# A transformer block on one core: how many expert tiles and steps of row maxima each first part gets

## The chip, the cores and the metric

The kernel runs on one core of one Trainium2 chip. The metric is the device time of one execution in microseconds, and its median over the runs. A profiled execution gives the trace from which the views below are taken; its own time is given beside its span.

## The reference

The program computes one block of a transformer with adaptive layer norm. The input x is (4, 2048, 256). With mod = silu(c) @ wmod cut into six rows per batch:

```python
h = layernorm(x) * (1 + ca) + sa
x = x + ga * attention(h)          # 8 heads of 32, causal, softmax over exact row maxima
h = layernorm(x) * (1 + cb) + sb
x = x + gb * experts(h)

# attention: scores = q k^T / sqrt(32) + head_scale * (q[:3].dir) (k[:3].dir)
# experts:   2 shared experts (256 -> 128 -> 256, gelu) for every token, and of 16 routed
#            experts the 4 with the largest softmax(h @ router_w^T), weighted by it
```

All is fp32.

## The kernel before

**Blocks.** The tokens are cut into 16 blocks of 512, four to a batch; qb = i % 4 is a block's place in its batch. A block's queries meet qb + 1 blocks of keys. Attention is done for one group of four heads at a time (NQ = 2 groups) and one key tile of 128 at a time, so block i has ks = 8 (qb + 1) such key tiles to sum, counted over both groups: 8, 16, 24 or 32.

**Maxima.** The exact maximum of every row of scores is found before the exponentials. `maxima(i)` (line 476) gives 8 (qb + 1) steps for a block. A step of `scores` (line 425) makes 4 matmuls of 128 queries by up to 512 keys into two PSUM tiles ps, which TensorE runs as 8; VectorE reduces each of the two tiles into parts, after adding the causal mask cmask to the last 128 columns where the diagonal crosses. The steps of the next block i + 1 are done during block i. Each step carries the time that it is expected to take on VectorE (M_VE = 2.7, and a little more at the start of a row of query tiles); M_US = 1.05 is what it is expected to take on TensorE (line 26).

**Two parts of a block.** The main loop (from the line `for i in range(NBLK)`) does each block in two parts. I call them F i and S i in this document.

- The first part, F i, is a list of pieces of TensorE work, each with a cost in microseconds: the projections of coming blocks (`project_steps`), the output projection of block i - 1 (`out_steps`, PSUM tiles po), the second norm's transposes, the router's logits and the shared experts of block i - 2 (`turn_steps`, `dense_steps`, tiles ptb, pl, pu and pd_s), and tiles of routed experts (`tile_steps`, tiles px, pu and py, four tiles of 128 rows at a time, whose weights wt are loaded by SP's queue). Among them stand steps of maxima of block i + 1.
- The sums, S i, go over the ks key tiles of block i: score matmuls (st), exponentials on ScalarE (p), and two matmuls with the probabilities, for the numerator (av) and the denominator (dv). What is left of the steps of maxima is spread over these key tiles, and VectorE's other work (norms, the router's choice, placing rows for experts) is put between them by `put`, in order, into the room of each key tile.

**The order of work is written out.** Each engine runs its instructions in the order in which the program issues them (class `Pinned`). In a first part, `fill_in` (line 517) decides that order. It keeps a clock t. A piece advances t by its cost. A step of maxima is issued as soon as t is at least free - 0.3 and advances t by M_US; free is then t plus the step's VectorE time. When less than 3 us of pieces is left, the remaining steps are issued one after the other. `fill_in` also calls `tick` at a fixed pace; a tick issues one indirect DMA of the routed experts (a scatter of rows to the experts' buffers, or a gather of results) on POOL, each held behind ScalarE's last instruction by `paced`.

**How much goes into a first part.** Before `fill_in` is called, the loop adds up own (the cost of its own pieces), whole (begin and the VectorE time of all steps of maxima of the next block) and backlog (the cost of all expert tiles that are ready). `take_tiles` takes tiles until the given sum is reached. Then m, the number of steps that are done in this part, is raised while the condition of the `while` loop holds; the rest goes to S i. The expert tiles come in five groups of blocks: [0, 1], [2, 3, 4], [5, 6, 7], [8, 9, 10], [11, 12, 13]. A group's tiles are ready when the last of its rows has been scattered. Blocks 14 and 15 are done at the end with the experts' weights resident.

**The router's choice.** `choice_steps` (line 856) works on the logits of block i - 2: differences to the row maximum, an exponential on ScalarE, shares, the four largest (`choose`), a rank of each row within its expert by small matmuls (`earlier_ones`, PSUM tile pk, which needs VectorE's selb), and weights. `place_steps` (line 1002), for the last block of a group, turns ranks into row addresses. In the kernel before both are put into S i, for every i above 1, ahead of the second norm of block i - 1 (its tiles mvb, rsb and xnb).

**PSUM.** The tiles ps, st and the like come in pairs of banks from a ring of three (`mring`); single banks come from two others (`accp`).

**Combining.** `combine` (line 1217) adds the four gathered rows of a token with their weights into a tile sum, which is stored to the output at the next combine.

Of the kernel before, what the change touches and what calls it, by code (L numbers as in the profile page):

```python
# [12 lines left out]
F32 = mybir.dt.float32  # L13
# [6 lines left out]
P = 128  # L20
# [5 lines left out]
T_US, P_US, M_US, M_VE, S_US = 0.6, 1.8, 1.05, 2.7, 3.2  # L26
# [66 lines left out]
def adaln_block_kernel(  # L93
# [14 lines left out]
    B, T, C = x.shape  # L108
# [34 lines left out]
    work = ctx.enter_context(tc.tile_pool(name="work", bufs=2))  # L143
# [346 lines left out]
    scatters = []  # L490
# [8 lines left out]
    def tick(add=True):  # L499
        for due in sums_due:  # L500
            due[0] -= 1
        if add and sums_due and sums_due[0][0] <= 0:
            sums_due[0][1].pop(0)()
            if not sums_due[0][1]:
                sums_due.pop(0)
        if scatters:
            scatters.pop(0)()
            return
        if not gathers and ready and len(sums_due) < 2:
            gathers.extend(ready[0][0])  # L510
        if gathers:
            gathers.pop(0)()
            if not gathers:
                sums_due.append([3, ready.pop(0)[1]])


    def fill_in(pieces, tops=(), begin=0.0, pace=3.2, add=False):

        pieces, tops = list(pieces), list(tops)
        t, free, turns, next_tick = 0.0, begin, [], 1.0
        while pieces or tops:
            if t >= next_tick:
                tick(add)
                next_tick = t + pace
            if tops and (t >= free - 0.3 or sum(us for us, _ in pieces) < 3.0):
                ve, steps, turn = tops.pop(0)
                t = max(t, free)
                for s in steps:  # L530
                    s()
                t += M_US
                free = t + ve
                if turn is not None:
                    turns.append([3, turn])
                continue
            us, step = pieces.pop(0)
            step()
            t += us
            if turns and us > 0.1:  # L540
                turns[0][0] -= 1
                if not turns[0][0]:
                    turns.pop(0)[1]()
                    t += T_US
        return [turn for _, turn in turns]

    def merged(one, other):

        placed = []
        for pieces in (one, other):  # L550
            at, total = 0.0, sum(us for us, _ in pieces)
            for us, step in pieces:
                placed.append(((at + us / 2) / total, (us, step)))
                at += us
        return [p for _, p in sorted(placed, key=lambda p: p[0])]


    with tc.tile_pool(name="setup", bufs=1) as setup:
# [98 lines left out]
        tops = maxima(1)  # L657
# [537 lines left out]
    def combine_steps(group):  # L1195

        n = group.n

        def gather(j, t, k, held):
            i = group.blocks[j]  # L1200
            at = i * QB + t * P
            if k == 0:
                held["got"] = work.tile([P, TOPK, C], F32, tag="got", name=f"got{i}_{t}")
                held["row"] = work.tile([P, C], F32, tag="row", name=f"row{i}_{t}")
                nc.sync.dma_start(out=held["row"], in_=pre[at : at + P])
            paced(
                nc.gpsimd.indirect_dma_start(
                    out=held["got"][:, k, :],
                    out_offset=None,
                    in_=yg[n % 2][: group.nt * P],  # L1210
                    in_offset=bass.IndirectOffsetOnAxis(
                        ap=group.at[:, j * TT + t, k : k + 1], axis=0
                    ),
                )
            )

        def combine(j, t, held):
            i = group.blocks[j]
            got = held["got"]
            while stores:  # L1220
                stores.pop(0)()
            acc = work.tile([P, C], F32, tag="sum", name=f"sum{i}_{t}")
            held["acc"] = acc
            weight = group.weight[:, j * TT + t]
            nc.vector.tensor_scalar(acc, got[:, 0, :], weight[:, 0:1], None, ALU.mult)
            for k in range(1, TOPK):
                nc.vector.scalar_tensor_tensor(
                    acc, got[:, k, :], weight[:, k : k + 1], acc, ALU.mult, ALU.add
                )

        def complete(j, t, held):
            i = group.blocks[j]
            at = i * QB + t * P
            acc, row = held["acc"], held["row"]
            nc.vector.tensor_tensor(acc, acc, gbs[:, i // NB, :], ALU.mult)
            nc.vector.tensor_tensor(acc, acc, row, ALU.add)
            stores.append(lambda: nc.sync.dma_start(out=of[at : at + P], in_=acc))

        out = []
        for j in range(len(group.blocks)):  # L1240
            for t in range(TT):
                held = {}
                out.append(
                    (
                        [partial(gather, j, t, k, held) for k in range(TOPK)],
                        [partial(combine, j, t, held), partial(complete, j, t, held)],
                    )
                )
        return out
# [126 lines left out]
    def group_of(i):  # L1376
        n = next(n for n, blocks in enumerate(GROUPS) if i in blocks)
        if len(groups) == n:
            groups.append(Group(n, GROUPS[n]))
        return groups[n]  # L1380

    def take_tiles(us):
        got = []
        while tiles_to_come and us > 0:
            got.append(tiles_to_come.pop(0))
            us -= got[-1][0]
        return got
# [16 lines left out]
    for i in range(NBLK):  # L1404
        b, qb = i // NB, i % NB
        ks = NQ * TT * (qb + 1)
        last = i + 1 == NBLK

        if i:
            soon, later = projected_in(i)  # L1410
            outs = out_steps(i - 1, oT)
            turns, ups, downs = [], [], []
            if i > 1:
                turns = turn_steps(i - 2)
                ups, downs = dense_steps(i - 2)
            begin = 5.0
            lead, mid = [], []
            if soon:
                new = project_steps(soon[0])
                lead = new[:2] + turns[:2] + new[2:6]  # L1420
                begin = sum(us for us, _ in lead) + 1.0
                mid = ups + turns[2:] + new[6:]
            elif later:
                new = project_steps(later[0])
                mid = new[:2] + turns[:2] + ups + new[2:3] + turns[2:] + new[3:]
            else:
                mid = turns[:2] + ups + turns[2:]
            if soon and later:
                mid += project_steps(later[0])
            finals = [s for two in zip(downs, outs) for s in two] if downs else outs  # L1430
            at = max(6, len(mid) - len(finals))
            tail = merged(mid[at:], finals) if mid[at:] else finals
            mid = mid[:at] + tail

            for n, s in enumerate(ends):
                (lead or mid).insert(2 * n + 1, (0.001, s))
            tops = [] if last else maxima(i + 1)
            state["pairs"] = not last
            own = sum(us for us, _ in lead + mid)
            whole = begin + sum(ve for ve, _, _ in tops)  # L1440
            backlog = sum(us for us, _ in tiles_to_come)
            now = take_tiles(1e9 if last else max(whole - own, backlog - 90.0))
            filler = own + sum(us for us, _ in now)
            m, busy = 0, begin
            while m < len(tops) and (
                busy + tops[m][0] <= filler + 2.0 or len(tops) - m > int(0.9 * ks)
            ):
                busy += tops[m][0]
                m += 1
            rest = tops[m:]  # L1450
            left = fill_in(lead + (merged(mid, now) if now and mid else mid), tops[:m], begin)
# [20 lines left out]
        for n, (_, ss, turn) in enumerate(rest):  # L1472
            at = int(0.93 * (n + 0.5) / len(rest) * ks)
# [33 lines left out]
            fresh = fresh[1:]  # L1507
        if i > 1:
            group = group_of(i - 2)
            steps = choice_steps(i - 2, group)  # L1510
            if i - 2 == group.blocks[-1]:
                steps += place_steps(group)
                filled = group
            put(steps, 1, 1)
        if i:
            steps = norm(second_norm_steps(i - 1))
# [15 lines left out]
        if 0 < i < 4:  # L1532
            now = tables[:3] if i == 1 else tables[:8]
# [25 lines left out]
    i, j = DENSE  # L1559
# [66 lines left out]
```

## Time and profile before

| | |
|---|---|
| median of 3 runs | 2571.34 us (2566.7 to 2572.5) |
| time of the profiled execution | 2561.29 us |
| its span | 2559.6 us |
| TensorE busy | 2397.4 us, 94% |
| VectorE busy | 1427.1 us, 56% |
| ScalarE busy | 981.4 us, 38% |
| POOL busy | 698.0 us, 27% |
| mean granted TensorE clock | 0.955 |

Busy time is the union of the durations of an engine's instructions. TensorE's matmuls are pipelined and their ends are modelled, so being busy does not mean that it works at its peak: a matmul that is held up or that runs at half the clock counts as busy too. That is why the lengths of the stages are compared in what follows, and not the busy shares. In the rows of the timeline, the first number is the start, the second how long the row lasted; x8 means that eight instructions of the same kind stand in it; the brackets name an idle time of the engine ahead of it and what ended it.

### The profile page before, as it was taken

The page shows a single profiled execution, that of the slowest core. Times are in us where ns is not written, and L with a number is a line of the kernel's source. Part 1 is how long each engine was busy: PE and PEld are TensorE (multiplying, and loading weights), DVE is VectorE, ACT ScalarE, POOL GpSimd, SP SyncE. Part 2 cuts the span into 40 slices and gives each one's busy share as a digit, 9 for nine tenths or more (in the row PEclk, how much of TensorE's full clock was granted, in tenths as well). Part 3 has the DMA queues.
Part 4 walks back from the last instruction along what each step waited for, and adds up shares of the span by engine and source line. Part 5 has one row for each costly group of instructions (what it writes and reads, how often), then busy time and mean ns, then how long its engine had stood idle before and what let it go on. Part 6 is the DMA issues. An engine that isn't in the chain of part 4 may idle for free. (4 is left out here: it accounts for less than half of the span.)

```text
span 2559.6 us, 42608 instructions
## 1 busy us (share of the span) xinstructions
PE 2397.4 (94%) x16961; PEld 1182.3 (46%) x16961; DVE 1427.1 (56%) x2833; ACT 981.4 (38%) x1391; POOL 698.0 (27%) x740
## 2 busy tenths in 40 slices
PE   7989999999999999999999999998999998998987
PEld 4443433345544333365645344364633257335754
DVE  5577665436667774346565656458557840422235
ACT  2324244543333344534343335533342343542420
POOL 3201010421124035201013333502353320354334
PEclk9989899999999899998999999998998999999999
DMA  2300403343532112233622135233623169338943
GB/s 87 118 1 9 148 9 109 115 132 116 163 114 67 34 44 99 73 115 122 211 95 75 50 126 179 82 129 112 221 90 109 56 200 300 110 121 278 325 136 116
DMA packets 219703, 306.91 MB, mean 120 GB/s; under 512 B 18544, under 2 KB 158832, under 8 KB 219504
## 3 DMA queue, kind: packets, MB, share of 16 engines
q1 hardware_dynamic: 192720, 228.89, 27.1%
q0 software_dynamic: 25536, 73.43, 9.0%
q8 instruction: 134, 2.20, 0.4%
q10 hardware_dynamic: 1248, 1.86, 0.2%
q14 instruction: 65, 0.53, 0.1%
HBM read 193.49 MB, written 114.82 MB: 120 GB/s over the span
## 5 line engine op out<-in xcount | busy, mean ns | idle before, releaser
L52 DVE TENSOR_REDUCE parts<-ps 128x2 f32<-128x1024 f32 (+3 forms) x640 | 662.4, 1063 | 318.4 <-PE ps L52 309.3
L52 ACT ACTIVATE p<-st 128x1024 f32<-128x1024 f32 (+3 forms) x640 | 538.6, 893 | 618.8 <-PE st L52 564.4
L52 PE MATMUL st<-qT,kv 32*128 32x512 f32 (+3 forms) x2560 | 412.0, 584 | 15.2 <-ACT p L52 7.6
L52 PE MATMUL ps<-kv,qT 32*128 32x512 f32 (+3 forms) x2560 | 400.8, 614 | 22.1 <-DVE parts L52 11.9
L52 POOL DMA_INDIRECT got<-yg,at x224 | 216.7, 968 | 368.5 <-ACT p L52 96.9
L52 PE MATMUL av<-p,kv 128*32 128x512 f32 (+3 forms) x2560 | 306.6, 549 | 3.8 <-ACT p L52 2.1
L52 PE MATMUL dv<-p,ones 128*32 128x512 f32 (+3 forms) x2560 | 302.3, 541 | 1.5 <-issue 1.5
L72 POOL DMA_INDIRECT xg<-rows,at x219 | 212.8, 972 | 299.5 <-ACT p L52 121.2
L52 PEld LDWEIGHTS st<-qT,kv 32*128 32x128 f32 x2560 | 143.9, 186 | 268.9 <-issue 196.2
L52 DVE TENSOR_TENSOR ps<-ps,cmask 128x256 f32<-128x256 f32 x256 | 109.3, 427 | 253.1 <-PE ps L52 208.6
L52 PEld LDWEIGHTS ps<-kv,qT 32*128 32x128 f32 x2560 | 135.0, 194 | 229.5 <-issue 90.2
L52 POOL TENSOR_TENSOR x<-x,tmps 128x512 f32<-128x512 f32 x28 | 35.4, 1264 | 519.8 <-DVE tmps L52 519.7
L52 PE MATMUL pu<-xt,wt 128*128 128x128 f32 x1216 | 161.3, 283 | 13.9 <-DMA wt<-experts 12.2
L52 PE MATMUL py<-wt,tact 128*128 128x256 f32 x608 | 163.6, 403 | 7.6 <-ACT xt L52 2.1
L52 PEld LDWEIGHTS pu<-xt,wt 128*128 128x128 f32 x1216 | 151.4, 195 | 37.1 <-issue 12.9
L52 PE MATMUL st<-mT,unit 3*128 3x512 bf16 (+3 forms) x1280 | 165.9, 348 | 0.0
L52 PEld LDWEIGHTS dv<-p,ones 128*32 128x32 f32 x2560 | 72.4, 110 | 174.0 <-issue 168.7
L52 ACT COPY y<-py 128x512 f32<-128x512 f32 x152 | 89.0, 585 | 144.1 <-PE py L52 141.5
L52 PEld LDWEIGHTS py<-wt,tact 128*128 128x128 f32 x608 | 111.1, 196 | 50.3 <-issue 9.0
L52 DVE RECIPROCAL rd<-rd 128x128 f32<-128x128 f32 x128 | 120.8, 943 | 0.8
L52 ACT COPY xt<-px 128x512 f32<-128x512 f32 x152 | 86.3, 586 | 85.2 <-PE px L52 82.1
L52 PEld LDWEIGHTS av<-p,kv 128*32 128x32 f32 x2560 | 52.6, 108 | 137.4 <-issue 112.4
(288 smaller groups left out, 2454.0 us busy)
## 6 DMA issues: line engine op xcount, KB each, us to landing
wt<-experts SPq DMA_DIRECT2D x304, 256.0 KB
xr<-xg SPq DMA_DIRECT2D x76, 512.0 KB
yg<-y SPq DMA_DIRECT2D x76, 512.0 KB
xg<-zeros SPq DMA_DIRECT2D x16, 1024.0 KB
xin<-in_x SPq DMA_DIRECT2D x16, 512.0 KB
x<-in_x SPq DMA_DIRECT2D x16, 512.0 KB
h2d<-xnb POOLq DMA_DIRECT2D x14, 512.0 KB
pre<-x POOLq DMA_DIRECT2D x14, 512.0 KB
```

The lines of the kernel that those rows point to most:

```text
L52: made = call(*args, **kwargs)
L72: made = call()
```

## The change

Six things are changed, all of them in the planning code.

- In `fill_in`, ticks follow each other after 2.2 us of its clock while there are scatters, and the next time is set ahead of the call.
- The tile sum has three buffers where the pool gave two.
- For the blocks with qb = 0 (i = 4, 8, 12) `choice_steps` of block i - 2 is merged into the pieces of the first part, two places behind the logits, at 0.05 us each, and is no longer put into the sums. `place_steps` stays in the sums.
- The time to be filled with tiles is reduced by M_US for each step of maxima, and the backlog up to which tiles may wait is 110 us where it was 90.
- The condition on m counts M_US for each step that was already taken, less 5 us, where it had a margin of 2 us.
- For qb = 0 all steps of maxima are done in the first part.

```diff
@@ fill_in
             if t >= next_tick:
+                next_tick = t + (2.2 if scatters else pace)
                 tick(add)
-                next_tick = t + pace
@@ combine
-            acc = work.tile([P, C], F32, tag="sum", name=f"sum{i}_{t}")
+            acc = work.tile([P, C], F32, bufs=3, tag="sum", name=f"sum{i}_{t}")
@@ main loop, first part
+            if i > 1 and qb == 0:
+
+                at = mid.index(turns[2]) + 2
+                steps = choice_steps(i - 2, group_of(i - 2))
+                mid[at:] = merged(mid[at:], [(0.05, s) for _, _, s in steps])
...
-            now = take_tiles(1e9 if last else max(whole - own, backlog - 90.0))
+            idle = whole - own - M_US * len(tops)
+            now = take_tiles(1e9 if last else max(idle, backlog - 110.0))
             filler = own + sum(us for us, _ in now)
             m, busy = 0, begin
+            most = 0 if qb == 0 else int(0.9 * ks)
             while m < len(tops) and (
-                busy + tops[m][0] <= filler + 2.0 or len(tops) - m > int(0.9 * ks)
+                busy + tops[m][0] <= filler + M_US * m - 5.0 or len(tops) - m > most
             ):
                 busy += tops[m][0]
                 m += 1
@@ main loop, sums
-            steps = choice_steps(i - 2, group)
+            steps = choice_steps(i - 2, group) if qb else []
```

## The prediction

> **What bounds the kernel now.** I read the page first, then a table of busy time by stage, then TensorE's timeline inside two stages. The page:
>
> ```profile
> span 2559.6 us, 42608 instructions
> PE 2397.4 (94%) x16961; PEld 1182.3 (46%) x16961; DVE 1427.1 (56%) x2833; ACT 981.4 (38%) x1391; POOL 698.0 (27%) x740
> PEclk9989899999999899998999999998998999999999
> ```
>
> TensorE is busy 94% of the span, VectorE 56%. The change adds no matmul and takes none away, so it can only alter how fast TensorE gets through its queue. I cut the span where a block's first score matmul (st) starts and its last denominator matmul (dv) ends: F i is the first part of block i, S i its sums. In each row, after the stretch: its length, then busy us of PE, PEld, DVE, ACT, POOL, the granted clock, DMA share, GB/s.
>
> ```profile
> 795.90:844.20 48.30, 44.82 (x196) 23.86 (x196) 33.20 (x42) 9.89 (x16) 10.28 (x10) 0.89 0.17 52
> 844.20:957.00 112.80, 110.57 (x893) 35.35 (x893) 82.26 (x159) 44.40 (x55) 28.59 (x31) 0.95 0.11 37
> 1189.60:1302.00 112.40, 105.38 (x624) 69.44 (x620) 71.63 (x100) 38.09 (x65) 13.40 (x15) 0.95 0.65 209
> 1302.00:1349.90 47.90, 47.02 (x501) 16.57 (x499) 27.35 (x92) 29.32 (x39) 10.97 (x14) 1.00 0.05 16
> 1401.60:1513.70 112.10, 109.75 (x893) 34.69 (x893) 67.94 (x119) 44.41 (x54) 40.42 (x44) 0.97 0.19 63
> 1561.40:1661.10 99.70, 98.37 (x947) 30.67 (x946) 55.31 (x152) 60.30 (x71) 49.49 (x52) 1.00 0.36 108
> 1763.20:1865.20 102.00, 89.74 (x508) 56.74 (x508) 68.53 (x105) 30.56 (x52) 35.44 (x38) 0.92 0.55 180
> ```
>
> These are F6, S6, F9, S9, S10, S11, F13. S11 holds 32 key blocks and no step of maxima: 99.7/32 = 3.12 us each. S10 holds 24 key blocks and 21 such steps: 112.1 - 24 x 3.12 = 37.3, so **a step costs 1.78 us in a sum**. S7, with five short steps, is 108.5 us: 8.8/5 = 1.76.
>
> What a step costs in a first part, TensorE's timeline of F6 shows (start, us):
>
> ```profile
> 822.24 1.14 PE L52 MATMUL ps<-kv,qT 32*128 32x512 f32 x8
> 823.31 1.99 PE L52 MATMUL pd_s<-wsh,act_-2_6212 128*128 128x256 f32 x8
> 825.14 1.89 PE L52 MATMUL pv<-wq,hT 128*128 128x256 f32 x8
> 826.97 1.99 PE L52 MATMUL ps<-kv,qT 32*128 32x512 f32 x12
> 829.42 1.83 PE L52 MATMUL ps<-kv,qT 32*128 32x512 f32 x8 [0.47 <-DVE parts L52]
> 831.68 0.70 PE L52 MATMUL ps<-kv,qT 32*128 32x256 f32 x4 [0.43 <-DVE parts L52]
> 832.81 7.76 PE L52 MATMUL ps<-kv,qT 32*128 32x512 f32 x24 [0.43 <-DVE parts L52]
> 840.50 3.73 PE L52 MATMUL po<-wo,oT 128*128 128x256 f32 x8
> ```
>
> Each step is 8 ps rows. Between other work it takes 1.07 us (822.24 to 823.31), and its two reductions (1221 ns each in the groups) run under the pieces that follow. When the pieces have run out, steps stand in a row: six from 826.97 to 840.50, 13.5 us, **2.26 us each**, at VectorE's pace. So there are three prices: 1.07 spread, 1.78 in a sum, 2.26 in a row. Granted clock in two such rows (F6 and F14):
>
> ```profile
> 827.00:840.50 13.50, 12.15 (x49) 4.42 (x48) 12.23 (x13) 0.59 (x1) 1.53 (x2) 0.75 0.28 87
> 1935.50:1954.60 19.10, 16.91 (x73) 7.10 (x72) 18.19 (x22) 0.00 (x0) 8.58 (x9) 0.73 0.38 122
> ```
>
> **The change, part by part.** *Allotment.* The new idle takes M_US off per step, so fewer tiles go into each first part; the new m adds M_US per step, so more steps do. fill_in is not changed: it still issues a step only when t reaches free, and free is the end of the step's matmuls plus its VectorE time. Each step thus still wants about 2.7 us of pieces. With fewer pieces per step the pieces run out earlier, and the rest of the steps stand in a row. I carried out the planner's arithmetic and read the order of matmuls on TensorE. Steps in each first part, in brackets those in a row at its end, and us of pieces:
>
> F4, F8: 16 (3), 63 -> 16 (6), 47. F5: 21 (3), 66 -> 21 (7), 53. F6: 11 (6), 26 -> 23 (8), 55. F9: 24 (3), 80 -> 21 (7), 53. F10: 11 (3), 34 -> 30 (12), 67. F12: 16 (2), 63 -> 16 (7), 46. F13: 21 (3), 66 -> 21 (8), 53. F14: 11 (9), 14 -> 29 (11), 67. F3, F7: 3 -> 1; F11: 8 -> 6 (short steps). F15 keeps 76 of 80 tile pieces.
>
> Tile pieces cost TensorE the same wherever they stand (F9: 112.4 less its steps is 83 for 80 planned), so moving them sums to nothing. They take their DMAs along: each set of four tiles has four weight loads of 256 KB, a row load and a store of 512 KB on SP's queue. They move from F9 (209 GB/s) to F10 and F14 (60 and 161 GB/s now); I cost it at 0, for F15 with 283 GB/s loses only some 10 us to late weights. If that cover fails the nearest row is those 10 us; below nothing, at most the same 10.
>
> Steps, all in us. Rows: 35 steps now, measured 73.1 in all (6.9 twice, 5.6, 13.5, 6.2, 5.8, 3.5, 5.6, 19.1). After: 72. Priced by VectorE's durations (2.28 a full step; with the causal edge 1.69 to 3.15) they make 165.8; short rows now cost up to 1.7 less than their VectorE sum and long ones none or 0.7, so I take 161: +88. Spread steps rise from 112 to 121: 9 x 1.07 = +10. From the sums 49 long steps go (12 in S6, 19 in S10, 18 in S14) and 3 come (S9): 46 x 1.78 = -82. Six short ones leave F3, F7 and F11 (0.63 each, -4) and come to S3, S7, S11 (1.76 each, +10.5). **Sum of the steps: +22.5.**
>
> *Clock.* After a row the last pieces run slow: po took 3.73 us at 840.50, against 1.99 for the same x8 of pd_s at 823.31. After the rows of F5, F10, F12 and F13, now two or three steps long, it shows no such slowing. Those four become long, and F6's gets one more piece behind it: some 1.8 for each, I take +8. The Trainium skill, "TensorE: Matmul & The Clock Gate", section "HAM oscillation — how this bites in real kernels", asks only for no TensorE gap over some 3.4 us; in the row at 827 no gap is over 0.47 us, and the clock still fell to 0.75. By the rule the term is 0 and the total +12; I go by the row. Ends: 0 and +15.
>
> *Choice.* choice_steps of blocks 2, 6 and 10 goes from S4, S8, S12 to F4, F8, F12: about 25 small VectorE instructions (some 5.5 us), one Exp, ten small pk matmuls and a copy. In S12 it stands ahead of place_steps on VectorE, and the second norm's power (rsb) comes behind both. F13 pays for it:
>
> ```profile
> 1775.65 0.48 PE L52 MATMUL ptb<-ident,xnb 128*128 128x128 f32 x1 [4.20 <-POOL xnb L52]
> ```
>
> Three more waits of 1.0 follow, 7.3 in all, under a half clock. Without the choice the chain starts some 5.5 us earlier: -6.5 in F13, -1 in S12. S4 and S8 gain nothing (TensorE idles 0.2 there). In F4, F8, F12 the Exp stands among Gelu tiles, and the program has six more table loads, 1.28 us each in the trace, 7.7 on ScalarE; copies that TensorE waits for stand behind. Half, +4. Queued behind pk are all of TensorE's pieces: if VectorE is late with selb, everything waits. Three steps lie between logits and need, so I take 0; ends 0 and +7 for each of three (the wait of F13).
>
> *Rest.* S14 costs 7 more than S10 now: 21 steps and nine combines on one VectorE (90.1 of 119.1). With 3 steps left: -5. F11's first row load waits 3.3; older tiles now stand ahead of it: -2. The third sum buffer: VectorE waits 34.8 for out<-sum, mostly in the end, where TensorE's gaps name other causes: 0; ends 0 and -3. Scatters every 2.2 instead of 3.2 (40 in F10) are 0.97 each on a POOL that is busy 18 of F10's 52: 0; a late POOL would show as x or xnb, up to +3.
>
> **Sum:** +22.5 + 8 - 7.5 + 4 - 5 - 2 = **+20 us**. The profiled execution took 2561.29 (span 2559.6 and 1.7 around it), so 2581. It lies 10 under the median of the runs, 2571.34; with that offset the forecast is 2591.
>
> **The rivals.** *A, faster: the rows cost less.* The new formula treats both engines as working side by side. If the steps in a row cost 1.66 (halfway between 1.07 and 2.26) the 72 make 120 instead of 161: 20 - 41 = -21, 2550. It decides at 20/72 = 0.28 less, about 1.96 us a step. For it: rows of three now stay under their VectorE sum. Against: at six, seven (16.1 in F1) and nine steps they don't, since the ps pairs are three, one and a half steps. *B, no change:* no clock term, no table loads, a little off the rows: about 2574. *C, much slower:* pk or the Exp holds up F4, F8 and F12 as the late norm holds up F13, 7 and a half-clock stretch of 3 each: 3 x 10 more, 2621. Against it: VectorE is busy only 48 of 85 us in F4, though 54 of 72 afterwards.
>
> **Numbers.** Forecast 0.62 (its own range 2578 to 2606), A 0.17, B 0.11, C 0.10. What a measurement here can tell from no change is about 0.2%, 5 us. A is faster, B counts as no change with a little of A's and the forecast's edges in balance, the rest is slower: 0.17, 0.10, 0.73. The range 2556 to 2616 leaves out the lower half of A and the upper half of C, and the far ends of the forecast.
>
> **What would show it.** Right: S10 near 78 us, S6 near 92, S14 near 82; F10 near 116, F14 near 110, F6 near 93; rows of 7 to 12 steps at 2.2 us, with the clock at about 0.75; F4 and F8 some 12 shorter, not 17; ptb's wait in F13 mostly gone. Wrong: rows under 1.9 us a step, or none; S5 and S9 much slower than 57 and 55; pk waiting over 2 us.

## The result, and the profile after

| | before | after |
|---|---|---|
| median of 5 runs | 2571.21 us (2566.7 to 2572.5) | 2584.65 us (2581.46 to 2586.71) |
| ratio to before | 1 | 1.0064 [1.0045, 1.0083] |
| profiled span | 2559.6 us | 2585.0 us |
| mean granted clock | 0.955 | 0.946 |

The change costs 0.64%. The profiled run of before lies 10 us below its median and that of after at the top of its runs, so the traces differ by 25.4 us where the medians differ by 13.4. The ratio, 0.64% or 16 us, is not that of the two medians (0.52%). The page of after:

```profile
span 2585.0 us, 42615 instructions
PE 2409.9 (93%) x16961; PEld 1195.0 (46%) x16961; DVE 1431.2 (55%) x2833; ACT 987.5 (38%) x1397; POOL 700.2 (27%) x740
PEclk9989899998999899999999899989899999998999
```

TensorE has the same number of matmuls and is busy 93% of the span in place of 94%; ScalarE has the six more instructions that the prediction named as table loads. So the answer is again in the stages. The first seven rows answer to those shown of before (F6, S6, F9, S9, S10, S11, F13); then come F10, F14, S14 and the end E, which is all that follows S15. The columns are those of before. The second table has F10, F14, S14 and E of before.

```profile
780.60:869.60 89.00, 84.28 (x456) 49.84 (x456) 62.14 (x75) 23.98 (x42) 4.57 (x4) 0.94 0.31 101
869.60:959.80 90.20, 88.30 (x798) 28.75 (x798) 53.00 (x123) 44.96 (x56) 40.61 (x44) 0.98 0.27 86
1183.50:1269.60 86.10, 79.97 (x441) 47.98 (x438) 58.09 (x76) 25.32 (x42) 6.30 (x7) 0.95 0.49 158
1269.60:1323.10 53.50, 52.58 (x524) 18.11 (x523) 34.19 (x98) 27.39 (x38) 10.99 (x13) 0.99 0.04 14
1442.40:1519.80 77.40, 76.48 (x739) 24.67 (x738) 22.88 (x65) 44.80 (x55) 14.77 (x17) 1.00 0.16 52
1552.90:1656.60 103.70, 102.85 (x963) 31.99 (x962) 60.38 (x159) 58.47 (x69) 56.11 (x59) 1.00 0.37 111
1754.20:1850.80 96.60, 84.99 (x443) 52.14 (x440) 66.93 (x100) 23.95 (x40) 36.36 (x38) 0.88 0.55 180
...
1323.10:1442.40 119.30, 111.24 (x588) 67.28 (x589) 81.15 (x100) 31.55 (x55) 44.24 (x45) 0.87 0.56 182
1905.20:2015.10 109.90, 104.32 (x616) 66.26 (x612) 77.96 (x95) 31.28 (x56) 13.56 (x13) 0.92 0.65 210
2015.10:2098.10 83.00, 79.26 (x748) 25.41 (x747) 48.20 (x120) 44.92 (x56) 40.72 (x44) 1.00 0.29 88
2303.80:2585.00 281.20, 233.81 (x1050) 164.12 (x1048) 103.01 (x230) 72.04 (x114) 109.37 (x115) 0.91 0.64 210
```

```profile
1349.90:1401.60 51.70, 48.28 (x235) 28.37 (x234) 32.11 (x38) 13.62 (x22) 17.92 (x18) 0.93 0.18 60
1920.50:1956.50 36.00, 33.02 (x152) 17.66 (x152) 31.50 (x38) 4.17 (x7) 15.21 (x15) 0.86 0.48 161
1956.50:2075.60 119.10, 114.23 (x893) 35.51 (x893) 90.10 (x172) 44.30 (x54) 39.82 (x43) 0.94 0.20 58
2288.00:2559.60 271.60, 231.39 (x1050) 163.42 (x1048) 102.97 (x230) 71.97 (x114) 109.10 (x115) 0.93 0.66 217
```

F6, F10 and F14 grew by 40.7, 67.6 and 73.9 us; S6, S10 and S14 shrank by 22.6, 34.7 and 36.1. F9 lost 26.3 and S9 gained 5.6. These are moves of steps and tiles, and most of them cancel. What does not cancel is how the steps stand in the first parts. TensorE's timeline at the end of F10 (start, duration; the brackets name the idle time ahead of the row and who ended it):

```profile
1410.26 1.13 PE L52 MATMUL py<-wt,tact 128*128 128x256 f32 x4 [0.29 <-ACT xt L52]
1411.32 1.35 PE L52 MATMUL ps<-kv,qT 32*128 32x512 f32 x12
1413.78 0.49 PE L52 MATMUL ps<-kv,qT 32*128 32x128 f32 x4 [1.11 <-DVE parts L52]
1414.91 23.36 PE L52 MATMUL ps<-kv,qT 32*128 32x512 f32 x80 [0.64 <-DVE parts L52]
1438.19 3.41 PE L52 MATMUL po<-wo,oT 128*128 128x256 f32 x8
```

From 1411.3 to 1438.2 TensorE issues nothing but ps: 96 matmuls, 8 to a step, so twelve steps in 26.9 us, 2.24 us each, at VectorE's pace. Nine first parts have such a row (F4, F5, F6, F8, F9, F10, F12, F13, F14), of 6, 7, 8, 6, 7, 12, 7, 8 and 11 steps: 72 steps in 159.8 us, where before had 35 in 73.1. Busy time and clock in the rows of F10, F14 and F4:

```profile
1411.30:1438.20 26.90, 25.15 (x98) 10.63 (x97) 25.49 (x30) 0.59 (x1) 10.59 (x11) 0.61 0.22 74
1986.30:2011.00 24.70, 22.68 (x89) 9.19 (x88) 23.95 (x28) 0.59 (x1) 8.95 (x9) 0.72 0.40 133
601.00:614.90 13.90, 12.57 (x50) 4.89 (x49) 12.53 (x16) 1.87 (x2) 0.00 (x0) 0.64 0.34 114
```

VectorE is busy 25.5 of 26.9 us in F10's row: it, not TensorE, sets the length, although TensorE too shows as busy. The granted clock is 0.61 to 0.72, and the po behind F10's row takes 3.41 us.

The other loss was not foreseen: E is 281.2 us where it was 271.6. TensorE in E, two rows of after, the row of before that answers to the second, and then two of after's scatters on POOL ahead of it:

```profile
2327.91 5.41 PE L52 MATMUL pd<-kv,act 128*128 128x256 f32 x16 [1.90 <-DVE act L52]
2347.37 1.94 PE L52 MATMUL px<-ident,xr 128*128 128x128 f32 x8 [14.05 <-DMA xr<-xg]
```

```profile
2325.18 1.94 PE L52 MATMUL px<-ident,xr 128*128 128x128 f32 x8 [8.11 <-DMA xr<-xg]
```

```profile
2321.02 0.96 POOL L72 DMA_INDIRECT xg<-rows,at  x1 [2.32 <-ACT gates L52]
2326.88 0.96 POOL L72 DMA_INDIRECT xg<-rows,at  x1 [4.90 <-ACT act L52]
```

The first routed tile of the end waits 14.05 us for its rows (8.11 before), and those rows wait for scatters that are held behind ScalarE's last instruction.

### The profile page after: what moved, and what is told of

Read it like the earlier page. It is cut to its first block, busy times and chain, and to the rows that moved or that the text cites. A ratio compares the mean times of both kernels' runs of the same rounds, so it can differ in the third digit from the quotient of the medians.

```text
span 2585.0 us, 42615 instructions
## 1 busy us (share of the span) xinstructions
PE 2409.9 (93%) x16961; PEld 1195.0 (46%) x16961; DVE 1431.2 (55%) x2833; ACT 987.5 (38%) x1397; POOL 700.2 (27%) x740
## 3 DMA queue, kind: packets, MB, share of 16 engines
q1 hardware_dynamic: 192720, 228.89, 26.9%
## 4 chain that ended last, share of the span: by engine, by line
PE 78%; DVE 8%; issue 4%; ACT 4%; DMA 3%; POOL 1%; another core or an unknown queue 1%; SPq 0%; POOLq 0%; ACTq 0%; DVEq 0%
PE st L52 16%; PE ps L52 14%; PE av L52 10%; PE dv L52 9%; PE pu L52 6%; PE py L52 5%; DVE parts L52 4%; PE po L52 2%; PE ppq L52 2%; DMA wt<-experts 2%; PE pv L52 2%; PE px L52 2%; PE ppk L52 2%; PE pd_s L52 2%; POOL got L52 1%
## 5 line engine op out<-in xcount | busy, mean ns | idle before, releaser
L52 PE MATMUL ps<-kv,qT 32*128 32x512 f32 (+3 forms) x2560 | 439.4, 649 | 26.4 <-DVE parts L52 19.3
L52 PE MATMUL st<-qT,kv 32*128 32x512 f32 (+3 forms) x2560 | 391.6, 582 | 12.9 <-ACT p L52 9.9
L52 PEld LDWEIGHTS ps<-kv,qT 32*128 32x128 f32 x2560 | 156.6, 203 | 250.7 <-issue 106.2
L52 PEld LDWEIGHTS st<-qT,kv 32*128 32x128 f32 x2560 | 132.7, 185 | 257.7 <-issue 192.0
L52 PE MATMUL py<-wt,tact 128*128 128x256 f32 x608 | 165.7, 404 | 10.9 <-ACT xt L52 3.2
L52 PE MATMUL st<-mT,unit 3*128 3x512 bf16 (+3 forms) x1280 | 152.4, 346 | 0.0
L52 DVE SCALAR_TENSOR_TENSOR sum<-got,weight,sum 128x256 f32<-128x256 f32 x168 | 84.3, 502 | 93.9 <-DMA got<-yg,at 81.7
L52 POOL TENSOR_TENSOR x<-x,tmp 128x512 f32<-128x512 f32 x32 | 41.0, 1283 | 316.9 <-DVE tmp L52 277.7
```

The costliest lines, as they stand in the source:

```text
L52: made = call(*args, **kwargs)
```

## The experiments

Each kernel has 5 to 12 runs. The chips differ (the medians of before were 2561.17 us for e1 to e4, 2554.78 for e5 to e8, 2550.49 for e9 to e12), so only the ratios to before on the same chip are compared. A ratio's interval, in brackets, reaches 0.15 to 0.3% to either side. The stages come from one profile of each kernel, and the clock alone moves them: S0 has the same matmuls in all fourteen kernels and is 32.7 us long in before and after, granted 1.00, but 37.3 in e11, granted 0.85. A stage's difference of up to some 5 us means little unless a wait or a second profile goes with it.

### Which part of the change costs what: e1, e2, e3

**e1: the change without the move of the choice.**

```diff
-            if i > 1 and qb == 0:
-                at = mid.index(turns[2]) + 2
-                steps = choice_steps(i - 2, group_of(i - 2))
-                mid[at:] = merged(mid[at:], [(0.05, s) for _, _, s in steps])
...
-            steps = choice_steps(i - 2, group) if qb else []
+            steps = choice_steps(i - 2, group)
```

> The changed kernel with choice_steps put back into the sums for every block; all else as changed. Rows theory (the loss is made by steps of maxima that stand one after the other at the end of a first part, at VectorE's pace): the rows stay (7, 7, 8, 7, 7, 12, 7, 8, 11 steps), so it stays slower than the kernel before, within 6 us of the changed kernel, 2579 to 2590. Choice theory (the router's choice among the pieces, with its wait of pk and its table loads, makes the loss): 2571 or less.

Measured: 2603.85 us, 1.0170 [1.0144, 1.0197]. Both expectations missed, on the same side: without the choice's move the change would cost 1.70%. The move is worth 1.06% in it, some 27 us. Where, TensorE's timeline at the start of F9 shows, first of e1, then of after:

```profile
1193.25 0.45 PE L52 MATMUL ptb<-ident,xnb 128*128 128x128 f32 x1 [0.90 <-DVE rd L52]
1193.94 0.47 PE L52 MATMUL ptb<-ident,xnb 128*128 128x128 f32 x1 [0.25 <-POOL xnb L52]
1195.43 0.48 PE L52 MATMUL ptb<-ident,xnb 128*128 128x128 f32 x1 [1.01 <-POOL xnb L52]
1196.91 0.47 PE L52 MATMUL ptb<-ident,xnb 128*128 128x128 f32 x1 [1.01 <-POOL xnb L52]
```

```profile
1188.08 0.63 PE L52 MATMUL ptb<-ident,xnb 128*128 128x128 f32 x4
```

In e1 the second norm is so late that its first four transposes are issued one by one, the last three each when POOL hands over its xnb. This is the wait that the prediction had seen in F13 alone. In after the four stand in one row without a wait. From the start of F5, F9 and F13 to the first ps TensorE takes 15.6, 15.4 and 19.9 us in e1, and 8.2, 8.2 and 14.9 in after. Against e1, after is shorter by 5.7 us in F5, 7.2 in F9, 6.3 in F13 and 2.5 in S12, together 21.7 of the 27. (The profiled spans differ by 11.5 only: S3 and E of after are 4.7 and 4.6 longer, stages whose work the edit leaves as it is.)

**e2: only the move of the choice, on the kernel before** (the same lines, added).

```diff
+            if i > 1 and qb == 0:
+                at = mid.index(turns[2]) + 2
+                steps = choice_steps(i - 2, group_of(i - 2))
+                mid[at:] = merged(mid[at:], [(0.05, s) for _, _, s in steps])
...
-            steps = choice_steps(i - 2, group)
+            steps = choice_steps(i - 2, group) if qb else []
```

> The kernel before with nothing but choice_steps moved to the first parts of blocks 4, 8 and 12. Rows theory: the rows of F4, F8 and F12 stay at two steps, S12 and F13 gain some 7, pk and the table loads take about 4 back: 2564 to 2574, no slower than before. Choice theory: 2580 or more.

Measured: 2535.06 us, 0.9902 [0.9876, 0.9928], a gain of 25 us where about nothing was expected. By stages of the two profiles: F13 -4.6 and S12 -2.0, near what was predicted, but also F5 -4.5, F9 -1.5, F10 -1.7, and F4 -4.2, F8 -4.5 and S4 and S8 -0.8 and -1.1, where the prediction had a cost or nothing. F4 and F5 of e2, and then of before:

```profile
535.90:616.60 80.70, 76.87 (x442) 48.71 (x442) 49.24 (x93) 32.02 (x52) 5.12 (x5) 1.00 0.51 169
637.90:726.40 88.50, 84.80 (x512) 54.46 (x508) 58.34 (x76) 30.62 (x52) 6.28 (x7) 1.00 0.49 159
```

```profile
536.80:621.70 84.90, 80.81 (x430) 50.01 (x428) 47.69 (x72) 29.12 (x48) 5.18 (x5) 0.96 0.50 163
643.80:736.80 93.00, 87.41 (x516) 56.02 (x512) 62.67 (x90) 30.74 (x52) 12.17 (x14) 0.96 0.48 152
```

Both are granted the full clock, where before had 0.96 in each. The two gain in different ways. F5, F9 and F13 gain at their start, as in the change: the first ps comes after 7.3, 8.5 and 14.6 us, where before took 11.8, 10.9 and 19.1. F4 and F8 gain at their end. The choice's pieces advance the clock of `fill_in` too, so one step more is spread, and the row is two steps long and not three. The last ps of F4's row and the po behind it, of before and of e2:

```profile
614.96 3.12 PE L52 MATMUL ps<-kv,qT 32*128 32x512 f32 x8 [0.21 <-DVE parts L52]
618.01 3.78 PE L52 MATMUL po<-wo,oT 128*128 128x256 f32 x8
```

```profile
613.62 1.13 PE L52 MATMUL ps<-kv,qT 32*128 32x512 f32 x4 [0.30 <-DVE parts L52]
614.68 1.99 PE L52 MATMUL po<-wo,oT 128*128 128x256 f32 x8
```

The row is 6.9 us long in before (from 611.1) and 3.5 in e2 (from 611.2); po takes 1.8 us less; the step that is now spread costs 1.0. Together that is F4's gain. So of the 25 us, some 11 lie ahead of the first ps of F5, F9 and F13, where the norm was waited for, and 8.7 in rows that became shorter by a step.

**e3: only the allotment, on the kernel before.**

```diff
-            now = take_tiles(1e9 if last else max(whole - own, backlog - 90.0))
+            idle = whole - own - M_US * len(tops)
+            now = take_tiles(1e9 if last else max(idle, backlog - 110.0))
...
+            most = 0 if qb == 0 else int(0.9 * ks)
...
-                busy + tops[m][0] <= filler + 2.0 or len(tops) - m > int(0.9 * ks)
+                busy + tops[m][0] <= filler + M_US * m - 5.0 or len(tops) - m > most
```

> The kernel before with nothing but the new idle, the backlog of 110 and the new condition on m. Rows theory: rows of 7 to 12 steps as in the changed kernel and no gain in F13: +15 to +28 against before, 2586 to 2599. Choice theory: the loss is gone, 2571 or less, since VectorE's idle time in the first parts takes the steps for nothing.

Measured: 2611.62 us, 1.0177 [1.0145, 1.0209]: 45 us, above the top of what was expected (28); its runs spread from 2595.7 to 2615.9. F5 and F9 of e3:

```profile
641.70:735.20 93.50, 84.58 (x436) 50.52 (x436) 62.30 (x89) 25.56 (x42) 12.15 (x14) 0.88 0.44 140
1195.30:1288.60 93.30, 83.54 (x436) 50.04 (x436) 62.31 (x89) 25.55 (x42) 12.17 (x14) 0.89 0.45 146
```

F5 has 13 us of pieces less than in before and takes 0.5 more; the prediction's steps and tiles had it 7.6 shorter. F9 is 19.1 shorter and not 25.5, F12 3.2 and not 10. S3, to which two short steps come, priced at 3.5, grew by 7.4. Together that is 25 us over the forecast. S3's part is not the steps': with the same matmuls S3 takes 114.3 us in e1, granted 0.99 and not 0.96. F5, F9 and F12 are as long in e1 as here. In F5 and F9, 3.7 and 4.5 us of the excess lie ahead of the first ps, which comes after 15.5 and 15.4 us. The clock in F5, F9, F12 and F13 fell to 0.88, 0.89, 0.89 and 0.83, from 0.96, 0.95, 1.00 and 0.92. Length times the share that was not granted is 11.2, 10.3 and 8.3 us in F5, F9 and F12, against 3.7, 5.6 and 0 in before: the clock can account for 20 of the 21 us that these three are over, at most, since in a row TensorE waits anyway. All of these stages follow or hold a row that became long, and the second norm is later: ptb waits 2.3, 2.3 and 9.0 us for xnb in F5, F9 and F13, where in before it waited 1.2, 0.4 and 7.3. That it is F4's and F8's long rows that leave VectorE late for the short S4 and S8 is argued and not shown by itself.

So by ratios: allotment +1.77%; pace and third buffer on top of it -0.07%; choice on top of both -1.06%; sum +0.64%. The second is within the intervals, and cannot be told from nothing.

### Is it the rows: e4, e5

**e4: the change, with TensorE's own time taken off the wait for VectorE.** `fill_in` sets free after t has already advanced by M_US. The edit starts VectorE's time with the step's matmuls, as the new idle and m assume.

```diff
-                free = t + ve
+                free = t + ve - M_US
```

> The changed kernel, with one line of fill_in changed: free = t + ve - M_US, so that a step's VectorE time is counted from its issue and not from the end of its matmuls. The same steps and nearly the same tiles stand in each first part, but spread: at the ends only 2, 2, 3, 2, 2, 5, 3, 0 and 5 steps are left in rows, 24 in place of 72. Rows theory: 48 steps at 1.07 in place of 2.26 and fewer slow clocks, -45 to -65 against the changed kernel, 2520 to 2540. If the rows are not the cause (VectorE or the pairs of ps banks are the bound however the steps are spread): within 10 us of the changed kernel.

Measured: 2514.41 us, 0.9825 [0.9799, 0.9852]; against after's 1.0064 that is 2.4%, 61 us, inside the 45 to 65 expected. The steps in the nine rows fall from 72 to 24. The line also shortens rows that the change had left as they were in before: F0 is 3.8 us shorter than in after and F2 6.2, 10 of the 61. F10 and F14 of e4, and then its timeline inside F10:

```profile
1279.80:1392.80 113.00, 106.25 (x590) 62.84 (x588) 82.07 (x102) 31.70 (x55) 40.30 (x42) 0.92 0.57 188
1836.50:1936.50 100.00, 93.82 (x570) 60.10 (x568) 72.44 (x90) 30.11 (x52) 8.74 (x8) 0.94 0.54 174
```

```profile
1364.82 1.14 PE L52 MATMUL ps<-kv,qT 32*128 32x512 f32 x8
1365.89 1.99 PE L52 MATMUL py<-wt,tact 128*128 128x256 f32 x8
1367.82 1.14 PE L52 MATMUL ps<-kv,qT 32*128 32x512 f32 x8
1368.88 2.05 PE L52 MATMUL pu<-xt,wt 128*128 128x128 f32 x16
```

One step, one piece of 2 us, one step: no wait, and the work between is done in VectorE's time. F10 is 6.3 shorter than in after with the same steps and tiles. (F14 isn't a like comparison: in e4 it has 27 steps and 64 px matmuls, in after 29 and 76, since three scatters of a group come only in F14.) The change's rows are thus not the price of the new allotment by itself, but of a new allotment on an issue rule that was not changed with it.

**e5: the same line on the kernel before.**

```diff
-                free = t + ve
+                free = t + ve - M_US
```

> The kernel before with the one line free = t + ve - M_US in fill_in and nothing else. Its rows shrink from 35 steps to 9 in F4 to F14 (3 in F6, 6 or 7 in F14, none elsewhere), and in F2 from 6 to 3. Rows theory: some 28 steps at 1.07 in place of about 2.1, and the slow clocks behind them, -20 to -40 against before. If what the change adds at the ends of first parts is not the rows: within 5 us of before.

Measured: 2526.31 us, 0.9888 [0.9868, 0.9909], 29 us, as expected. F6 is 3.8 shorter, F10 6.3, F2 6.2, F4 and F8 4.5 each; F11 and F12 give 11.3 and 5.1 back (in F11 the first px waits 6.5 us for its rows, 3.3 in before, and the clock is 0.86 and not 0.93). The line helps without the allotment too, half as much: before had half as many steps in rows. With the line on both sides, the whole change is thus worth 0.9825 against 0.9888, 0.6%.

### What the prediction had costed at nothing: e6, e9, e10

**e6: only the pace of 2.2 us and the third buffer, on the kernel before.**

```diff
+                next_tick = t + (2.2 if scatters else pace)
                 tick(add)
-                next_tick = t + pace
...
-            acc = work.tile([P, C], F32, tag="sum", name=f"sum{i}_{t}")
+            acc = work.tile([P, C], F32, bufs=3, tag="sum", name=f"sum{i}_{t}")
```

> The kernel before with the tick pace of 2.2 while there are scatters and the third buffer of sum, and nothing else. My prediction put both at 0 (ends -3 and +3). Second thought, from the order of instructions: the scatters of the group of blocks 8 to 10 are then all issued in S13, not one late, so that its 80 tile pieces stand in F14 and not in F15, with all 32 steps of maxima of block 15 spread among them: 21 steps leave S14 (-37, and -5 for its combines), F14's row falls from 9 to 3 and 21 more steps come (+16), F15 loses its waits for weights (-10 to -13): about -38. Against it the last fill_in, whose pace was 1.3, becomes slower to scatter: +6 in the end. Sum -25 to -40. If a group's moment does not matter: within 5 us.

Measured: 2509.00 us, 0.9816 [0.9792, 0.9840], 47 us, more than the 25 to 40 expected. F14, S14, F15 and E of e6:

```profile
1907.70:2041.90 134.20, 128.51 (x840) 87.65 (x836) 85.22 (x101) 49.71 (x88) 9.64 (x9) 0.99 0.75 246
2041.90:2114.80 72.90, 72.02 (x723) 23.21 (x722) 41.86 (x114) 44.78 (x55) 40.74 (x44) 1.00 0.40 117
2114.80:2129.00 14.20, 13.39 (x65) 10.17 (x65) 7.47 (x12) 4.18 (x7) 5.75 (x6) 1.00 0.10 29
2229.30:2508.20 278.90, 233.38 (x1051) 163.91 (x1048) 102.93 (x230) 71.99 (x114) 108.77 (x115) 0.92 0.65 211
```

F14 grew by 98.2, S14 and F15 shrank by 46.2 and 96.4: 44 us net. With faster scatters a group's last rows are there before F14 is planned (three of its scatters come in F14 of before, none in F14 of e6), its tiles become pieces of F14 instead of F15, and the steps of maxima stand between them at full clock instead of in S14. E is 7.3 longer. In the change itself this gain is not to be had: there older tiles, left over by the smaller idle and the higher backlog, fill F14 already (64 px matmuls stand in F14 of e3, none in before's).

**e9: the change without the third buffer.**

```diff
-            acc = work.tile([P, C], F32, bufs=3, tag="sum", name=f"sum{i}_{t}")
+            acc = work.tile([P, C], F32, tag="sum", name=f"sum{i}_{t}")
```

> The changed kernel with two buffers of sum, as before. The waits of VectorE for out<-sum come back, mostly in the end, where TensorE waits for other things: the same as the changed kernel, between 0 and +4 us against it (1.003 to 1.009 of before). If the third buffer carries part of what the pace seemed to give: +8 or more.

Measured: 2560.32 us, 1.0034 [1.0017, 1.0051], within what was expected, though on another chip than after's 1.0064; E is 277.3 and the wait of px 13.5. The kernel is not slower without the buffer, so its 0 stands. (Alone on the kernel before, it wasn't tried without the pace.)

**e10: the change with a pace that is never longer than the one it replaces.** In E the old pace was 1.3 us, so 2.2 is slower there.

```diff
-                next_tick = t + (2.2 if scatters else pace)
+                next_tick = t + (min(2.2, pace) if scatters else pace)
```

> The changed kernel with min(2.2, pace) while there are scatters, so that the fill_in of the end, with its pace of 1.3, scatters as before. In the changed kernel its last eleven scatters come 6 us late and the first load of expert rows after them makes TensorE wait 14.1 us in place of 8.1: -5 to -8 against the changed kernel (0.999 to 1.004 of before). If that wait is chance: no change.

Measured: 2555.90 us, 1.0018 [1.0002, 1.0034]. The row of TensorE in E that answers to the one of after:

```profile
2312.56 1.73 PE L52 MATMUL px<-ident,xr 128*128 128x128 f32 x7 [9.82 <-DMA xr<-xg]
```

The wait is 9.82 us instead of 14.05, and E 269.4 instead of 281.2 (277.3 in e9). The other profiles say the same. In the five kernels with 2.2 in the end (after, e1, e4, e6, e9) E is 276.6 to 282.6 us and this wait 12.9 to 15.1; in the nine with 1.3 E is 269.4 to 275.2 and the wait 7.7 to 9.8. So 2.2 in the end costs some 7.5 us, the difference of the means. The ratio is 0.16% below e9's on the same chip; their intervals overlap.

### Is the late norm the whole of the choice's gain: e11

**e11: the kernel before, with the second norm ahead of the choice in S4, S8 and S12.**

```diff
-        if i > 1:
+        for norm_now in ((True, False) if qb == 0 else (False, True)):
+            if not norm_now and i > 1:
...
                 put(steps, 1, 1)
-        if i:
+            if norm_now and i:
...
```

> The kernel before with one order changed: in the sums of blocks 4, 8 and 12 the second norm is put into the key tiles ahead of the router's choice (and of place_steps) and not behind. No work moves to a first part and no row changes. If the choice's gain of 26 comes from the second norm that it held up, F5, F9 and F13 gain 4 to 8 each as in the kernel with the choice alone: -8 to -18. If it comes from the pieces' order in F4, F8 and F12 and their rows of two: within 4 us of before; place_steps coming later could cost up to 3.

Measured: 2555.81 us, 1.0018 [1.0002, 1.0033]: no gain, where 8 to 18 us were expected. The norm does come in time: ptb no longer waits for xnb, and the first ps of F5, F9 and F13 comes after 8.6, 8.5 and 14.4 us, 10 us earlier in all than in before. But S4, S8 and S12 are 5.4, 4.6 and 4.5 longer. TensorE in S12:

```profile
1764.07 0.20 PE L52 MATMUL pk<-selb,earlier 128*128 128x16 bf16 x1 [4.59 <-DVE selb L52]
```

Now the choice is late, and pk holds up everything queued behind it. In neither order do the short sums hold both chains without a wait; moving one of them out is what gains.

### A version that beats both: e7, e8, e12

**e7: everything but the allotment.** Before, with the choice's move of e2, the third buffer, the line of e5 and the pace of e10.

```diff
+                next_tick = t + (min(2.2, pace) if scatters else pace)
                 tick(add)
-                next_tick = t + pace
...
-                free = t + ve
+                free = t + ve - M_US
```

> The kernel before with the choice in the first part, the third buffer, the pace min(2.2, pace) while there are scatters, and free = t + ve - M_US; the allotment stays as before. Rows theory: there is enough filler for every step, so rows vanish but for F1, F2 and F6; choice -26 as measured alone, rows -20 to -30 (part of it is in the -26), group in F14 -30 to -40: -70 to -100 against before, the fastest so far. If the new allotment is what made the spread kernel fast, this one lies above its 0.9825.

Measured: 2471.16 us, 0.9686 [0.9663, 0.9708], 80 us, within the 70 to 100 expected. F14 is 140.7, S14 72.5, F15 14.2 and E 272.0.

**e8: e4 with a pace of at most 1.9 us**, to see whether the allotment is as good once its other costs are gone.

```diff
-                next_tick = t + (2.2 if scatters else pace)
+                next_tick = t + (min(1.9, pace) if scatters else pace)
...
-                free = t + ve
+                free = t + ve - M_US
```

> The changed kernel with free = t + ve - M_US and the pace min(1.9, pace) while there are scatters, so that the group of blocks 8 to 10 is ready before F14 and the last fill_in scatters at 1.3 again. Rows 2 to 5 steps. Against the same kernel without the pace (0.9825 of before): the end -6, F14 and F15 -5 to -10: 0.975 to 0.982 of before. If the new allotment is the better one once steps are spread, it is faster than the kernel with the old allotment and everything else; the prices of a step (1.07 spread, 1.78 in a sum) say it could be by up to 15 us, less what its rows of 5 in F10 and F14 cost and what the long F14 gains in the other.

Measured: 2480.45 us, 0.9724 [0.9701, 0.9747], slightly better than expected. F15 is 102.9 long, 11.6 of it idle, at 302 GB/s: TensorE waits 9.9 us for weights there (wt), which the tiles that were put off bring with them.

**e12: e8, with block 14 taking every tile that is ready.**

```diff
-            now = take_tiles(1e9 if last else max(idle, backlog - 110.0))
+            now = take_tiles(1e9 if i + 2 >= NBLK else max(idle, backlog - 110.0))
```

> The kernel with the new allotment, free = t + ve - M_US and the pace min(1.9, pace) (0.9724 of before), with one more change: block 14 takes all tiles that are ready, as block 15 does. F14 then holds 149 us of pieces with all 32 steps spread and no row (5 of 12 us now), S14 loses 3 steps (-5), F15 its waits for weights (-11): -15 to -22 against that kernel, 0.964 to 0.967 of before, the fastest. If weights in F14 then come late instead: no gain.

Measured: 2472.47 us, 0.9687 [0.9666, 0.9709]; a little less gain than expected. F14 is 187.8 with no row, F15 14.2. That is e7's ratio within the intervals: with the issue rule put right and the tiles not put off to F15, no difference between the two allotments can be told.

## Why the prediction was right, and where two of its terms were not

The forecast was +20 us on the profiled execution; the medians moved by 13.4 and the ratio gives 16. The rows' mechanism was right, and so was their size. That the total came out as near was luck: two other terms were mis-sized by about the same amount, some 22 us, in opposite directions.

- **Steps in rows: right.** 161 us for 72 steps were forecast, 159.8 measured, 2.22 each. S10, S6, S14 were to be near 78, 92, 82 and are 77.4, 90.2, 83.0; F10, F14, F6 near 116, 110, 93 and are 119.3, 109.9, 89.0. Rival A, rows under 1.96 us a step, is out, and rival B, no change, is outside the ratio's interval; e4 shows the rows' worth from the other side. The clock in the rows was said to be about 0.75 and was 0.61 to 0.72.
- **Allotment as a whole: mis-sized.** Steps, clock, S14 and F11 together were some +23.5; e3 measured +45. The step that failed is "Clock ... I take +8" and what stands beside it: each row was priced by itself, with a short slow piece behind it. The runs show more: F5, F9, F12 and F13 are granted 0.83 to 0.89, and the second norm is waited for longer in the first parts behind the long rows. The mean clock of e3's span is 0.937 over 2614.2 us, of before's 0.955 over 2559.6. In the traces the granted clock is either full or half, so e3 spends 329 us at half clock and before 230. Half of the 99 more bounds what it can cost. How the missing 22 us are shared between clock and waiting stays open.
- **Choice: mis-sized.** "-6.5 in F13, -1 in S12" was near (-4.6 to -6.3, and -2.0 to -2.5). "S4 and S8 gain nothing" was near right of the stages themselves (-0.8, -1.1), but the norm that they delay is waited for at the start of F5 and F9, as F13 waits behind S12, and there it was not looked for: 7 us between before and e2, and 15 between e1 and after. The "+4" for table loads and the Exp is +0.8, 0 and +0.8 in F4, F8 and F12 between e1 and after; on the kernel before F4 and F8 gained 4 each, by a shorter row. In all -25 to -27 where -3.5 was said. F4 and F8, which were to be some 12 shorter in after, are 8.4 and 10.4 shorter.
- **pk: right.** It waits 1.4 us in F4 and F8 of after, under the 2 that were named, and not at all in F12. Rival C did not come.
- **Third buffer at 0: right** (e9). **Pace at 0: wrong twice.** It was weighed as POOL's busy time. In E the pace rises from 1.3 to 2.2 us, which makes the scatters late: some 7.5 us over all profiles, and most of E's 9.6. And on the kernel before, pace and buffer are worth 47 us (e6) through the time at which a group's tiles become ready; with the allotment no such effect can be told, -0.07% on top of it.
- **Tiles at 0: nothing speaks against it in the change**, though no run tests it alone; F15, with a few pieces less, is 5.9 us shorter.
- **The rule of the clock gate.** The Trainium skill, "TensorE: Matmul & The Clock Gate", section "HAM oscillation — how this bites in real kernels", asks for no gap over some 3.4 us; by that alone the clock's term would be 0. In F10's row the longest gap shown is 1.11 us and the clock is 0.61. The measurement decides; the prediction went by the row and was still too low.

## What to carry to other kernels

A planner's sum and its issue rule must hold the same model: this change planned as if two engines worked side by side, on an issue loop that still ran them one after the other, and one line in that loop turns +0.64% into -1.75%, some 0.4% of it on rows that were there before. When a wait is found in one place of a periodic schedule (F13), look for it in each place that has the same period (F5, F9), and look again after an edit that makes the engine ahead of it later. A pace is weighed by what becomes ready in time, not by the busy time of the queue that carries it.

## What the runs showed of the hardware that was not expected

The granted clock falls inside a row of ps matmuls that wait for VectorE although no gap is over 1.11 us: 0.61 over F10's 26.9 us, 0.72 over F14's 24.7, 0.64 over F4's 13.9. It stays low for a few microseconds of dense work behind the row (po: 3.41 us for x8). With the rows spread, as in e4, the mean clock of the span is 0.965, against 0.946 in after. The clock also differs from one execution to another where the program does not: S0, with the same matmuls, was granted 1.00 in before and 0.85 in e11, and took 32.7 and 37.3 us.
